# The forget gate's products with the tokens, for two sequences at once, by half-width blocks

## The chip, the cores and the metric

The kernel runs on one core of a Trainium2 chip. The metric is the device time of one execution, in microseconds (us). PE is the matrix engine; its weight loads are listed as PEld and run beside its products. DVE is VectorE, ACT is ScalarE, POOL is GpSimd, and SP issues most of the DMAs. A product here is one matrix instruction: a 128x128 stationary operand (loaded by its own weight load) times a moving operand of up to 512 columns, added up in a PSUM bank. A bank holds 128x512 numbers of 32 bits.

## The reference, cut to what matters

The whole computation is a mixture-of-experts stage, a feed-forward stage chosen by sequence, a second mixture of experts, and a gated recurrence. Only the last one is touched. For x of 32 sequences ("steps" of the scan), each with 128 rows of 512 numbers:

```python
def step(c, xt):
    ft = jax.nn.sigmoid(xt @ wf.T + c @ uf.T + bf)
    it = jax.nn.sigmoid(xt @ wi.T + c @ ui.T + bi)
    gt = jnp.tanh(xt @ wc.T + c @ uc.T + bc)
    c = ft * c + it * gt
    return (c, None)
c_final, _ = lax.scan(step, c0, x)
h = jnp.tanh(jnp.einsum('tbi,oi->tbo', x, wo) + c_final @ uo.T + bo)
return h
```

The input of the scan is r * y: the expert rows y, gathered by token, times sigmoid(r).

## The kernel before

**Precision.** Each 32-bit operand is split into a high part (a cast on ACT) and a remainder (a subtraction on DVE) by `split` (L64, L65). A product of two split operands is made of three products: high by high, high by rest, rest by high (`mm3`, L95). A contraction over 512 numbers has four chunks of 128, so it takes 12 products; over 256 numbers it takes 6.

**The scan** is the loop over t from 0 to 31 near the end of the kernel. Each t multiplies the state c, turned by PE (`turn`) and split into cT, by uc, ui and uf (`from_c`, 36 products of 512 columns into three banks of the pool ps_g). `gate` then adds the token's part, and applies the sigmoid or tanh; `new_c` makes f*c + i*g on DVE, and the next state is turned again. The token parts do not depend on the state. They are placed between `new_c` and the next `from_c`, as filler: some before the turn, while DVE and ACT make the new state, and some behind the turn, while ACT and DVE split it.

**Blocks.** For gates c and i, the token parts of two sequences (a pair n: tokens 2n and 2n+1) are made together. The left operand is seen as 2x2 blocks A11, A12, A21, A22 (sequence by half of the 512 inputs), the right operand as 2x2 blocks (half of the inputs by gate c or i). Instead of eight block products seven are made (Winograd's form of Strassen's method): of A11, A12, A22 and four sums S1 to S4 of A blocks, with B11, B21, B22 and four differences T1 to T4 of B blocks. Each takes 6 products of 512 columns into one of three banks of the pool ps_bF (`block`), and DVE adds the results up. `first_of_pair` makes five of them at odd t, for the even token t+1; `second_i` and `second_c` make the other two at even t. The first pair is done per token, from the block weights (`plain`).

**The forget gate f before the change** is plain: 12 products of 512 columns a token, added to the bank in which `from_c` then puts the state's part.

**Preparing tokens.** `gate_y(b)` multiplies y by sigmoid(r), turns it (ptF), stores it to DRAM for the last stage, and splits it into z; `sums_z` makes S1 to S4 on DVE once both tokens of a pair are there. `get_y` gathers y on POOL's queue and loads r on SP's. The loop does token t+3 at step t.

**Weights.** uc and ui come first, then uf, wc and wi, late in the expert stage. wf comes on POOL's queue during the first products of the scan; the second half of the block weights (`rest_of_weights`) is made at t=0 behind the split of the first new state.

**The end.** Behind the scan wo multiplies all tokens again, four sequences at a time (`unit`, results poF), and the last state's part uo (cu) is added; tanh, an addition and a store follow (`result`). The wo split is at t=28; the uo split is behind the scan.

**Order.** Dependences, semaphores and buffers are handled by a tile framework. Its planner goes through the program and gives each engine, at every point of its own estimate of time, the earliest instruction in the program whose operands and buffer it takes to be ready. So an engine's order is the program's unless something earlier waits: at 2318.57 us the first units of the end stand ahead of the last state's turn. Once it is set, each engine works its list strictly in order. `tc.issue_after` and `queue_behind` put an instruction behind another on the same engine without a wait.

Of the kernel before, what the change touches and what calls it, by code (L numbers as in the profile page):

```python
# [49 lines left out]
def tile_kernel(ctx: ExitStack, tc: tile.TileContext, a: dict, out: bass.AP):  # L50
# [106 lines left out]
    hl = const.tile([P, KD, NB], F32, name="hl")  # L157
# [18 lines left out]
    with ExitStack() as sa:  # L176
# [653 lines left out]
        new_i = po_p.tile([P, NB], I32, name="new_i")  # L830
        ones = po_p.tile([P, P], F32, name="ones2")
# [734 lines left out]
    with sf:  # L1566
# [35 lines left out]
        zp = sf.enter_context(tc.tile_pool(name="zp", bufs=2, **kw))  # L1602

        zA, zS, zts = {}, {}, {}

        def gate_y(b):
# [6 lines left out]
            if j == 0:  # L1613
                z = zp.tile([P, 2 * KD * D], FR, tag="z", name=f"z_{n}")
                zA[n] = z[:, : KD * D].rearrange("p (j h k q) -> p j h k q", j=2, h=2, k=KD)
                zS[n] = z[:, KD * D :].rearrange("p (s h k q) -> p s h k q", s=4, h=2, k=K2)
                zts[n] = first_p.tile([P, 2, KD, P], F32, tag="cT0", name=f"zt_{n}")
# [5 lines left out]
            zt = zts[n][:, j]  # L1623
            if b < LEAD:
                split(zA[n][:, j, 0], zA[n][:, j, 1], pt)
# [3 lines left out]
            if b >= LEAD:  # L1629
                split(zA[n][:, j, 0], zA[n][:, j, 1], zt)  # L1630

        def sums_z(n):
# [3 lines left out]
            s = gp.tile([P, 2, K2, P], F32, tag="sz", name=f"sz_{n}")  # L1636
# [7 lines left out]
        def turn(c, t):  # L1644
            pt = ps_c.tile([P, KD, P], F32, tag="t", name=f"ptC_{t}")
            for k in range(KD):
                nc.tensor.transpose(pt[:, k, :], c[:, bass.ts(k, P)], ident)
# [6 lines left out]

        def block(which, w, n):

            s = {"A11": (0, 0), "A12": (0, 1), "A22": (1, 1)}.get(which)
            if s is None:
                left = zS[n][:, int(which[1]) - 1]
            else:  # L1660
                left = zA[n][:, s[0], :, s[1] * K2 : (s[1] + 1) * K2]
            ps = ps_b.tile([P, D], F32, tag="b", name=f"p{which}_{n}")
            mm3(ps, lambda h, k: left[:, h, k, :], lambda h, k: wt[w][:, h, bass.ts(k, D)], K2)
            return ps

        def plain(t, ps, which, start, stop):
# [5 lines left out]
                "f": ((0, "f0"), (1, "f1")),  # L1672
# [3 lines left out]
            for m, (half, w) in enumerate(todo):  # L1676
                z = zA[n][:, j, :, half * K2 : (half + 1) * K2]
# [6 lines left out]
        half_done, made = {}, []  # L1684

        def first_of_pair(n):

            first, second, c1 = (zop.tile([P, 2, D], F32, tag="raw", name=f"{x}_{n}") for x in ("ta", "tb", "pa"))
            p1, u, v = first[:, 0], first[:, 1], second[:, 0]
            nc.vector.tensor_tensor(p1, block("A11", "B11", n), bias["c"], ALU.add)  # L1690
# [27 lines left out]
        def gate(t, n, ps, v, more):  # L1718
            v[n] = gp.tile([P, D], F32, tag="v" + n, name=f"v_{n}_{t}")
# [5 lines left out]
        def new_c(t, v, c):  # L1725
# [5 lines left out]

        wt = {
            n: wx_p.tile([P, 2, K2 * D], FR, tag="w" + n, name=f"w{n}_hl")
            for n in ("T4", "T3", "T2", "f1", "B22", "T1", "B21", "B11", "f0")
# [167 lines left out]
        for o in range(KD):  # L1902
            unit(0, o)
# [117 lines left out]
```

## Time and profile before

| | us |
|---|---|
| median of three executions | 2417.46 (2416.41 to 2418.44) |
| the profiled execution's own time | 2420.01 |
| its span, first to last instruction | 2418.3 |
| scan, 1781.3 to 2318.3: PE busy | 535.7 of 537.0 |
| scan: DVE busy, ACT busy | 339.6, 169.2 |
| one steady pair of tokens (start of ps_c at 1898.40 to 1931.61) | 33.2 |
| DVE busy in a steady pair (2000.41 to 2033.62) | 20.8 |
| after the scan, 2318.3 to 2418.3: PE busy | 93.6 of 100.0 |

The granted clock of PE is 1.00 in the scan. A row of the profile names the line, the engine, the operation, its output and inputs by the program's names, the shapes and a count. Matrix instructions overlap in their records, so the distance between the starts of two rows tells what a product costs, not its own duration (388 ns for 512 columns, 279 ns for 256). DVE takes 0.69 us for an addition of 128x512 and 0.42 us for one of 128x256.

### The profile page before, as it was taken

The numbers are of one execution on the slowest core, as the hardware profiler recorded it, in microseconds if no ns is written. First come the engines' busy times: TensorE is split into PE (matmuls) and PEld (weight loads), VectorE is DVE, ScalarE is ACT, GpSimd is POOL, SyncE is SP. The second block draws the span as 40 slices with busy tenths as digits, with TensorE's granted clock in tenths as the row PEclk, the third lists the DMA queues.
The fourth block names the chain that finished last, engine by engine and source line by source line (L and its number), as shares of the span: only waits on it lengthen the run. The fifth ranks groups of instructions, "written<-read, shape, count | busy, mean of one in ns | idle before, by whom it ended". The sixth has DMA issues, their size and how long they took to land.

```text
span 2418.3 us, 36797 instructions
## 1 busy us (share of the span) xinstructions
PE 2392.4 (99%) x12792; PEld 2026.3 (84%) x12792; DVE 1484.2 (61%) x2548; ACT 1077.0 (45%) x1897; POOL 422.4 (17%) x461
## 2 busy tenths in 40 slices
PE   9999999999999999999999999999999999999999
PEld 6788788888887888888888889999988888888887
DVE  8896644456557445446355477776756666666664
ACT  5544533343223545445455466666643223223242
POOL 1000022222233233323222120000011000000012
PEclk9999999999999999999999999999999999999999
DMA  6545555457565344343243287777642111111175
GB/s 220 152 128 171 183 170 167 153 184 254 178 216 164 126 129 127 106 133 109 81 153 125 90 288 257 224 229 232 199 153 65 49 44 53 49 44 48 53 235 183
DMA packets 196382, 357.93 MB, mean 148 GB/s; under 512 B 37664, under 2 KB 70480, under 8 KB 193632
## 3 DMA queue, kind: packets, MB, share of 16 engines
q1 hardware_dynamic: 148224, 258.57, 32.8%
q0 software_dynamic: 36448, 75.95, 11.0%
q10 hardware_dynamic: 11520, 20.98, 2.4%
q8 instruction: 107, 1.75, 0.3%
q14 instruction: 83, 0.68, 0.1%
HBM read 377.08 MB, written 91.80 MB: 194 GB/s over the span
## 4 chain that ended last, share of the span: by engine, by line
PE 76%; DVE 2%; DMA 2%; issue 1%; ACT 1%; ACTq 0%; SPq 0%; POOL 0%; DVEq 0%; POOLq 0%
PE po L95 7%; PE phD L95 7%; PE poD L95 7%; PE ps_f L95 7%; PE p L95 6%; PE pb L95 4%; PE ps_i L95 4%; PE ps_c L95 4%; PE poF L95 3%; PE pS L95 3%; PE pv L95 3%; PE acc L95 3%; PE pA L95 2%; PE pur L95 2%; PE por L95 2%
## 5 line engine op out<-in xcount | busy, mean ns | idle before, releaser
L65 DVE TENSOR_TENSOR wD<-rawD,wD 128x1024 fp32r<-128x1024 f32 x128 | 156.3, 1228 | 79.2 <-ACT wD L64 79.1
L95 PE MATMUL p<-xhl,swu 128*128 128x512 f32 x768 | 188.4, 397 | 5.9 <-ACT xhl L64 5.9
L95 PE MATMUL p<-xhl,kept_u 128*128 128x512 f32 x768 | 184.6, 394 | 1.3 <-DVE kept_u L65 0.7
L95 PEld LDWEIGHTS phD<-xe,wD 128*128 128x128 f32 x1536 | 183.2, 188 | 1.3
L95 PE MATMUL phD<-xe,wD 128*128 128x256 f32 x1536 | 183.5, 279 | 0.0
L95 PE MATMUL poD<-wD,hD 128*128 128x512 f32 x768 | 181.9, 392 | 0.7 <-DVE hD L65 0.7
L95 PEld LDWEIGHTS p<-xhl,swu 128*128 128x128 f32 x768 | 144.2, 190 | 36.1 <-ACT xhl L64 5.9
L95 PEld LDWEIGHTS p<-xhl,kept_u 128*128 128x128 f32 x768 | 141.8, 188 | 31.4 <-DVE kept_u L65 1.1
L95 PEld LDWEIGHTS poD<-wD,hD 128*128 128x128 f32 x768 | 141.8, 188 | 29.4 <-DVE hD L65 1.2
L64 ACT CAST wD<-rawD 128x1024 fp32r<-128x1024 f32 x128 | 133.4, 1047 | 54.3 <-PE poD L95 30.8
L305 POOL DMA_INDIRECT xg<-in_x_rows_dram,blk_t x71 | 68.2, 961 | 439.0 <-PE ptx L315 242.8
L1587 POOL DMA_INDIRECT y<-res_d,gat_i x32 | 37.1, 1158 | 471.3 <-DVE r L1612 388.3
L95 PE MATMUL pur<-r,xb 128*128 x792 | 110.6, 288 | 3.5 <-issue 1.5
L65 DVE TENSOR_TENSOR xb<-ptx,xb 128x512 fp32r<-128x512 f32 x68 | 47.0, 691 | 104.5 <-ACT xb L64 101.7
L95 PE MATMUL por<-r,hbr 128*128 x396 | 107.6, 407 | 0.5 <-ACT hbr L64 0.5
L95 PEld LDWEIGHTS pur<-r,xb 128*128 128x128 f32 x792 | 98.5, 188 | 5.6 <-issue 2.4
L95 PE MATMUL ps_c<-uc_hl,cT 128*128 128x512 f32 x384 | 96.3, 399 | 0.0
L95 PE MATMUL pb<-rT,Wo_hl 128*128 128x256 f32 x768 | 94.7, 281 | 0.3 <-DVE rT L65 0.2
L95 PE MATMUL acc<-swd,as 128*128 128x512 f32 x384 | 94.5, 391 | 0.2 <-DVE as L65 0.2
L95 PE MATMUL ps_f<-wf_hl,z 128*128 128x512 f32 x384 | 94.5, 394 | 0.0
L95 PE MATMUL acc<-kept_d,as 128*128 128x512 f32 x384 | 93.6, 392 | 0.8 <-ACT as L64 0.4
L844 POOL DMA_INDIRECT o<-o_d,s_i x64 | 64.5, 1008 | 165.4 <-PE pth L864 71.3
(1048 smaller groups left out, 5137.2 us busy)
## 6 DMA issues: line engine op xcount, KB each, us to landing
rawD<-in_w_key_dram SPq DMA_DIRECT2D x64, 512.0 KB
rawD<-in_w_value_dram SPq DMA_DIRECT2D x64, 512.0 KB
swr<-in_sw_dram SPq DMA_DIRECT2D x120, 256.0 KB
o_d<-obr SPq DMA_DIRECT2D x66, 256.0 KB
rraw<-in_rw_dram SPq DMA_DIRECT2D x32, 256.0 KB
xc<-in_x_dram SPq DMA_DIRECT2D x32, 256.0 KB
hid_d<-o ACTq DMA_DIRECT2D x32, 256.0 KB
xh_d<-xc SPq DMA_DIRECT2D x32, 256.0 KB
```

The source lines that it names most:

```text
L64: first = nc.scalar.copy(hi, src).ins
L65: done = nc.vector.tensor_tensor(lo, src, hi.bitcast(F32), ALU.subtract).ins
L95: done = nc.tensor.matmul(ps, lhsT=left(hl, k), rhs=right(hr, k), start=start and k + n == 0, stop=stop and 3 * k + n == last,)
L305: nc.gpsimd.indirect_dma_start(out=xg[i], out_offset=None, in_=a["x_rows"], in_offset=bass.IndirectOffsetOnAxis(ap=blk_t[:, i : i + 1], ax ...
L844: nc.gpsimd.indirect_dma_start(out=o[n], out_offset=None, in_=o_d, in_offset=bass.IndirectOffsetOnAxis(ap=idx[:, b : b + 1], axis=0),)
L1587: got = nc.gpsimd.indirect_dma_start(out=y, out_offset=None, in_=res_d, in_offset=bass.IndirectOffsetOnAxis(ap=gat_i[:, b : b + 1], axis=0),)
```

## The change

The f gate's token part is made by the same seven blocks. The left blocks are those of the pair, already there for c and i. The right operand is wf alone, its 512 columns cut in two halves: f11, f12, f21, f22 (half of the inputs by half of the columns), with differences T1 to T4 of their own. So each block product is 6 products of 256 columns, and two of them share a bank (`blocks_f`).

- `f_start(n)` makes A11 and A12 of f for pair n. It is run at even t for the next pair (at t=1 for the first one), ahead of the turn; DVE adds its results behind the state's split.
- `f_first(n)` makes S1, S2 and S4 at odd t, behind the turn; its additions go behind the new state.
- `f_second(n)` makes S3 at even t ahead of the turn, and `f_third(n)` makes A22 behind the turn and behind the c block.
- `plain_f` does tokens 0 and 1 one by one, 30 products of 256 columns each, from the block weights.
- The token part of f now reaches the gate as a tile in SBUF (`fs`), as those of c and i did; the state's product with uf starts its own bank.
- The wf weights are prepared as seven half-width blocks in one tile, which starts 64 bytes off (`shifted`); the raw wf lies in the buffer that S1 to S4 of the tokens use later, which has a single copy now.
- The block A21 of a token pair is no longer split except for the first pair. `sums_z` uses the gathered y tile as its scratch, so the next `get_y` comes behind it.
- At the end, the two pools of the scan are closed at t=30 instead of behind the loop. The wo split moves to t=30; two of the four loads of the first group's tokens go to another buffer at t=28 and two are at t=30; the uo split goes behind the last new state, the second group's split behind the first's, and the last state's turn behind the second unit of wo.
- A small tile (hl) moves from a lasting pool to one of an earlier stage.

```diff
         def gate_y(b):
             n, j = divmod(b, 2)
             with tc.issue_after(last_split[1]) if b == 1 else nullcontext():
                 nc.vector.tensor_tensor(r, y, r, ALU.mult)
             if j == 0:
-                z = zp.tile([P, 2 * KD * D], FR, tag="z", name=f"z_{n}")
-                zA[n] = z[:, : KD * D].rearrange("p (j h k q) -> p j h k q", j=2, h=2, k=KD)
-                zS[n] = z[:, KD * D :].rearrange("p (s h k q) -> p s h k q", s=4, h=2, k=K2)
+                zA[n] = zp.tile([P, 3, 2, K2, P], FR, tag="z", name=f"z_{n}")
                 zts[n] = first_p.tile([P, 2, KD, P], F32, tag="cT0", name=f"zt_{n}")
...
+            def split_tokens(t):
+                if j == 0:
+                    t = t.rearrange("p (a k) q -> p a k q", a=2)
+                    split(zA[n][:, 0:2, 0], zA[n][:, 0:2, 1], t)
+                    return
+                if n == 0:
+                    a21.append(gp.tile([P, 2, K2, P], FR, tag="a21", name="a21"))
+                    split(a21[0][:, 0], a21[0][:, 1], t[:, :K2])
+                split(zA[n][:, 2, 0], zA[n][:, 2, 1], t[:, K2:])
...
         def sums_z(n):
             zt = zts[n]
             a1, a2 = zt[:, 0, :K2], zt[:, 0, K2:]
             b1, b2 = zt[:, 1, :K2], zt[:, 1, K2:]
-            s = gp.tile([P, 2, K2, P], F32, tag="sz", name=f"sz_{n}")
+            zS[n] = zp.tile([P, 4, 2, K2, P], FR, tag="zs", bufs=1, name=f"zs_{n}")
+            s = spare[2 * n + 1].rearrange("p (s k q) -> p s k q", s=2, k=K2)
             nc.vector.tensor_tensor(s[:, 0], b1, b2, ALU.add)
             nc.vector.tensor_tensor(s[:, 1], s[:, 0], a1, ALU.subtract)
             split(zS[n][:, 0:2, 0], zS[n][:, 0:2, 1], s)
...
+        def left_of(which, n):
+            if which[0] == "S":
+                return zS[n][:, int(which[1]) - 1]
+            return tokens(n, int(which[1]) - 1, int(which[2]) - 1)
...
+        def blocks_f(n, *todo):
+
+            ps = ps_b.tile([P, 2, HD], F32, tag="b", name=f"pf{todo[0][0]}_{n}")
+            for i, (which, w) in enumerate(todo):
+                left = left_of(which, n)
+                mm3(ps[:, i], lambda h, k: left[:, h, k, :], lambda h, k: wf[w][:, h, k, :], K2)
+            return ps
+
+
+        fs, f_done = {}, {}
+
+        def f_tile(t):
+            pool, tag = (gp, "vf") if t % 2 or t == 0 else (first_p, "c0")
+            fs[t] = pool.tile([P, D], F32, tag=tag, name=f"v_f_{t}")
+            return fs[t][:, :HD], fs[t][:, HD:]
+
+        def plain_f(t):
+            n, j = divmod(t, 2)
+            f_tile(t)
+            ps = ps_b.tile([P, 2, HD], F32, tag="b", name=f"pf_{t}")
+            for i, todo in enumerate((((0, "B11"), (1, "B21")), ((0, "B11"), (0, "T1"), (1, "B22")))):
+                for m, (half, w) in enumerate(todo):
+                    z = tokens(n, j, half)
+                    done = mm3(
+                        ps[:, i], lambda h, k: z[:, h, k, :], lambda h, k: wf[w][:, h, k, :], K2,
+                        m == 0, m == len(todo) - 1,
+                    )
+            nc.vector.tensor_tensor(fs[t], ps.rearrange("p i n -> p (i n)"), bias["f"], ALU.add)
+            return done
+
+        def f_start(n):
+
+            f1, p1 = f_tile(2 * n)
+            ps = blocks_f(n, ("A11", "B11"), ("A12", "B21"))
+            return [
+                nc.vector.tensor_tensor(p1, ps[:, 0], bias["f"][:, :HD], ALU.add).ins,
+                nc.vector.tensor_tensor(f1, ps[:, 1], p1, ALU.add).ins,
+            ]
+
+        def f_first(n, room):
+
+            u, v = room[:, :HD], room[:, HD:]
+            p1 = fs[2 * n][:, HD:]
+            ps = blocks_f(n, ("S1", "T1"), ("S2", "T2"))
+            last = blocks_f(n, ("S4", "B22"))
+            with tc.issue_after(made[0]):
+                nc.vector.tensor_tensor(v, ps[:, 0], bias["f"][:, HD:], ALU.add)
+                nc.vector.tensor_tensor(u, ps[:, 1], p1, ALU.add)
+                nc.vector.tensor_tensor(v, v, u, ALU.add)
+                nc.vector.tensor_tensor(p1, last[:, 0], v, ALU.add)
+            f_done[n] = u, v
+
+        def f_second(n):
+            f1, f2 = f_tile(2 * n + 1)
+            u, v = f_done.pop(n)
+            ps = blocks_f(n, ("S3", "T3"))
+            adds = [
+                nc.vector.tensor_tensor(u, ps[:, 0], u, ALU.add).ins,
+                nc.vector.tensor_tensor(f2, ps[:, 0], v, ALU.add).ins,
+            ]
+            return (f1, u), adds
+
+        def f_third(n, f1, u):
+            nc.vector.tensor_tensor(f1, blocks_f(n, ("A22", "T4"))[:, 0], u, ALU.add)
...
         def first_of_pair(n):
 
             first, second, c1 = (zop.tile([P, 2, D], F32, tag="raw", name=f"{x}_{n}") for x in ("ta", "tb", "pa"))
             p1, u, v = first[:, 0], first[:, 1], second[:, 0]
+            rooms[n] = second[:, 1]
...
         def gate(t, n, ps, v, more):
-            v[n] = gp.tile([P, D], F32, tag="v" + n, name=f"v_{n}_{t}")
+            v[n] = fs.pop(t) if n == "f" else gp.tile([P, D], F32, tag="v" + n, name=f"v_{n}_{t}")
...
+        names = ("T4", "T3", "T2", "B22", "T1", "B21", "B11")
+        f_all = shifted(wx_p, len(names) * K2 * D, tag="wf", name="wf_hl")
+        f_all = f_all.rearrange("p (w h k n) -> p w h k n", w=len(names), h=2, k=K2)
+        wf = {n: f_all[:, i] for i, n in enumerate(names)}
         wt = {
             n: wx_p.tile([P, 2, K2 * D], FR, tag="w" + n, name=f"w{n}_hl")
-            for n in ("T4", "T3", "T2", "f1", "B22", "T1", "B21", "B11", "f0")
+            for n in names
         }
...
         for n in "cif":
-            from_c(0, n, ps, cT, True, False)
-
-
-        f01 = zp.tile([P, 2 * KD * D], F32, tag="z", name="raw_wf")
-        f01 = [f01[:, bass.ts(h, K2 * D)] for h in range(2)]
+            from_c(0, n, ps, cT, True, n == "f")
+
+
+        raw_f = zp.tile([P, KD, D], F32, tag="zs", bufs=1, name="raw_wf")
         with tc.issue_after(first_got):
             for h in range(2):
-                nc.gpsimd.dma_start(out=f01[h], in_=a["wf"].rearrange("p k n -> p (k n)")[:, bass.ts(h, K2 * D)])
+                s = slice(h * K2, (h + 1) * K2)
+                nc.gpsimd.dma_start(out=raw_f[:, s], in_=a["wf"][:, s])
...
         with behind(first_z):
-            for h in range(2):
-                split_part(f"f{h}", f01[h])
+            split_f("B11", f11)
+            split_f("B21", f21)
+            nc.vector.tensor_tensor(f12, f12, f11, ALU.subtract)
+            split_f("T1", f12)
+            split_f("B22", f22)
...
+            nc.vector.tensor_tensor(f22, f22, f12, ALU.subtract)
+            split_f("T2", f22)
+            nc.vector.tensor_tensor(f11, f22, f11, ALU.subtract)
+            nc.vector.tensor_tensor(f21, f21, f22, ALU.subtract)
+            split_f("T3", f11)
+            split_f("T4", f21)
...
                 with tc.issue_after(done):
-                    plain(0, ps, "f", False, True)
+                    plain_f(0)
+                more["f"] = fs[0]
                 for n in "cif":
                     gate(t, n, ps, v, more[n])
             else:
+                more["f"] = fs[t]
                 for n in "cif":
                     from_c(t, n, ps, cT, n not in ps, True)
...
             if t == 1:
 
                 nc.vector.tensor_tensor(bias["i"], bias["i"], bias["c"], ALU.subtract)
+                b1, b2 = (bias["f"][:, bass.ts(i, HD)] for i in range(2))
+                nc.vector.tensor_tensor(b2, b2, b1, ALU.subtract)
             n, odd = divmod(t + 1, 2)
             if t == 0:
                 for w in "ci":
                 cT_next = turn(c, t + 1)
                 with behind(last_split):
                     rest_of_weights()
-                plain(1, ps, "f", True, False)
+                plain_f(1)
             elif t < NB - 1:
                 if odd:
                     second_i(n)
-                    plain(t + 1, ps, "f", True, False)
+                    rest, adds = f_second(n)
+                    if n + 1 < NB // 2:
+                        adds += f_start(n + 1)
                 else:
                     first_of_pair(n)
+                    if n == 1:
+                        f_start(n)
                 cT_next = turn(c, t + 1)
                 if odd:
+
+                    for i in adds:
+                        queue_behind(i, last_split[1])
                     second_c(n)
+                    f_third(n, *rest)
                 else:
-                    plain(t + 1, ps, "f", True, False)
+                    f_first(n, rooms.pop(n))
...
                 gate_y(b)
+                if b % 2:
+                    sums_z(b // 2)
+                spare.pop(b)
                 if b + LEAD < NB:
                     get_y(b + LEAD)
-                if b % 2:
-                    sums_z(b // 2)
...
             if t == NB - 4:
-
-                wo1 = zp.tile([P, 2, KD, D], FR, tag="z", name="wo_hl")
+                raws = []
                 for k in range(KD):
-                    raw = yp.tile([P, D], F32, tag="yr"[k % 2], name=f"raw_wo{k}")
+                    raws.append(yp.tile([P, D], F32, tag="yr"[k % 2], name=f"raw_wo{k}"))
                     with tc.issue_after(last_r[0]):
-                        nc.sync.dma_start(out=raw, in_=a["wo"][:, k, :])
+                        nc.sync.dma_start(out=raws[k], in_=a["wo"][:, k, :])
+                first_z = first_p.tile([P, 2, KD, P], F32, tag="cT0", name="zr_0")
+                first_z = [first_z[:, j] for j in range(2)]
+                for j in range(2):
+                    nc.sync.dma_start(out=first_z[j], in_=z_d[0][j])
+            if t == NB - 2:
+
+                sx.close()
+                sz.close()
+                op = sf.enter_context(tc.tile_pool(name="op", bufs=1, side="right", **kw))
+                zp = sf.enter_context(tc.tile_pool(name="z0p", bufs=1, **kw))
+                uo1 = op.tile([P, 2, KD * D], FR, tag="uo", name="uo_hl")
+                wo1 = op.tile([P, 2, KD, D], FR, tag="wo", name="wo_hl")
+                for k, raw in enumerate(raws):
                     split(wo1[:, 0, k], wo1[:, 1, k], raw)
-                first_z = []
-                for j in range(GB):
+                for j in range(2, GB):
                     first_z.append(yp.tile([P, KD, P], F32, tag="yr"[j % 2], name=f"zr_0_{j}"))
                     nc.sync.dma_start(out=first_z[j], in_=z_d[0][j])
-        sx.close()
-        op = sf.enter_context(tc.tile_pool(name="op", bufs=1, side="right", **kw))
...
         split_z(0)
-        uo1 = op.tile([P, 2, KD * D], FR, tag="uo", name="uo_hl")
-        for h in range(2):
-            s = bass.ts(h, K2 * D)
-            split(uo1[:, 0, s], uo1[:, 1, s], raw_part("uo", h))
+        first_z = tuple(last_split)
+        with behind(first_z), tc.issue_after(made[0]):
+            for h in range(2):
+                s = bass.ts(h, K2 * D)
+                split(uo1[:, 0, s], uo1[:, 1, s], raw_part("uo", h))
...
-        for o in range(KD):
-            unit(0, o)
+        ahead = [unit(0, o) for o in range(KD)]
+        for i in turned_c:
+            queue_behind(i, ahead[1])
...
         for g in range(NG):
             if g + 1 < NG:
-                split_z(g + 1)
+                with behind(first_z) if g == 0 else nullcontext():
+                    split_z(g + 1)
```

## The prediction

> **What bounds the kernel now.** First the page's head, its table of busy time, and one group of instructions:
>
> ```profile
> span 2418.3 us, 36797 instructions
> PE 2392.4 (99%) x12792; PEld 2026.3 (84%) x12792; DVE 1484.2 (61%) x2548; ACT 1077.0 (45%) x1897; POOL 422.4 (17%) x461
> ...
> L95 PE MATMUL ps_f<-wf_hl,z 128*128 128x512 f32 x384 | 94.5, 394 | 0.0
> ```
>
> The matrix engine (PE) is busy in 99% of the span. The change rewrites the 384 products of the third line. They lie in the scan, 1781 to 2318 us. So the second view is PE's timeline over one steady token there (column one is the start, column two the extent of the row):
>
> ```profile
> 2003.36 2.88 PE L95 MATMUL ps_f<-uf_hl,cT 128*128 128x512 f32 x12
> 2006.08 1.52 PE L95 MATMUL pS<-wT_hl,z 128*128 128x512 f32 x6
> 2007.44 2.89 PE L95 MATMUL ps_f<-wf_hl,z 128*128 128x512 f32 x12
> 2010.16 0.60 PE L1647 MATMUL ptC<-ident,c 128*128 128x128 f32 x4
> 2010.52 1.64 PE L95 MATMUL pA<-wT_hl,z 128*128 128x512 f32 x6
> 2011.99 0.60 PE L1620 MATMUL ptF<-ident,r 128*128 128x128 f32 x4
> 2012.35 3.01 PE L95 MATMUL ps_c<-uc_hl,cT 128*128 128x512 f32 x12
> ```
>
> No row has a wait. The extents overlap, so a product costs the distance of starts: 12 in 2.72 us, 226.7 ns each. The same view in the expert stage prices a 256-column product, which the change will use:
>
> ```profile
> 1620.12 11.47 PE L95 MATMUL phD<-xe,wD 128*128 128x256 f32 x96
> 1631.43 2.92 PE L95 MATMUL poD<-wD,hD 128*128 128x512 f32 x12
> ```
>
> 96 in 11.31 us: 117.8 ns, which is 52% of 226.7, not 50%. Third, what the filler between the state's products covers. VectorE (DVE) in the same token:
>
> ```profile
> 2008.39 0.69 DVE L1728 TENSOR_TENSOR c<-v_f,v_i 128x512 f32<-128x512 f32 x1
> 2009.00 0.68 DVE L1705 TENSOR_TENSOR ta<-pS,ta 128x512 f32<-128x512 f32 x1
> 2009.60 0.68 DVE L1706 TENSOR_TENSOR pd<-pS,tb 128x512 f32<-128x512 f32 x1
> ...
> 2011.41 0.69 DVE L65 TENSOR_TENSOR cT<-ptC,cT 128x512 fp32r<-128x512 f32 x1 [1.13 <-ACT cT L64]
> ```
>
> The new state is ready at 2009.08 and PE turns it at 2010.16, its weight load 0.23 earlier: 0.85 us to spare. Queued 512-column additions start 0.60 apart. Last, the start of the scan, where DVE is full, and PE's only wait of the scan, from the table of waits:
>
> ```profile
> 1809.81 0.69 DVE L65 TENSOR_TENSOR cT<-ptC,cT 128x512 fp32r<-128x512 f32 x1 [1.98 <-ACT cT L64]
> ...
> 1825.96 0.68 DVE L1690 TENSOR_TENSOR ta<-pA,bc_bc 128x512 f32<-128x512 f32 x1
> ...
> 1826.70 1.65 PE L95 MATMUL pS<-wT_hl,z 128*128 128x512 f32 x6 [0.21 <-DVE ta L1690]
> ```
>
> ```profile
> PE pS L95 <- DVE ta L1690: 0.2, 1, 0.2
> ```
>
> There PE waited for a PSUM bank of the block pool (three banks), which `ta` frees.
>
> **The change, part by part.** The profiled execution took 2420.01 us (span 2418.3), 2.55 above the median of three; I sum differences against it and set them on the median.
>
> *Products of pairs 1 to 15.* Out go 2 × 12 products of 512 columns: 24 × 0.2267 = 5.44 us a pair. In come 7 blocks of 6 products of 256 columns: 42 × 0.1178 = 4.95. That is 0.49 × 15 = **−7.4 us**, all on the path because PE never idles.
>
> *The rule against it.* The Trainium skill, "TensorE: Matmul & The Clock Gate", section "Back-to-back issue gap", gives sustained spacings of about 131 ns for 512 columns and 81 for 128 in streams of weight load and product; in between, 256 would cost an estimated 98, and 42 × 98 against 24 × 131 would be a loss of 0.97 us a pair, 14.6 in all. This trace has 226.7 and 117.8, so the change wins by the trace; only the rule's direction remains, that a narrower product costs more per column.
>
> *Seams.* A 512-column row straight after 256-column ones took 2.76 instead of 2.72 (from 1631.43 to 1634.19). One to three such seams a pair, 0.04 each: 0.6 to 1.8; I take one, since two of the three meet transposes, which cost what they did: **+0.6**.
>
> *The first pair* stays per token but by the block weights, 12 + 18 products of 256 columns: 60 × 0.1178 = 7.07 against 5.44: **+1.6**, half of it before the first turn of the state.
>
> *Weights of f.* Out: two casts and two subtractions of 1024 columns on ACT and DVE. In: seven of each of 512 columns, and four subtractions of whole blocks. The first four with one subtraction lie at 1793 to 1799, where DVE idled 0.95 and 0.79 us before its two rows for wf: nothing; uncovered, 0.6. The last three with three subtractions, (3 + 3) × 0.60 = 3.6 us of DVE, go behind the state's split at 1810, into the full queue shown above.
>
> *What that delays.* `ta` must come behind 3.6 of weights, 0.60 (the plain f sum of token 1), 0.34 (the bias difference; 128x256 ones in the queue are 0.34 apart, as 1822.89 and 1823.22), less 0.26 for half a token split: 4.3, and DVE starts 0.8 later because PE turns later. So `ta` ends at 1826.64 + 5.1 = 1831.7. PE ends the state's products 1.6 later than now, at 1822.5, and has banks for A11, A12 (2.72) and the new two-block start (1.41), then four transposes (0.36): 1827.0. Wait 4.7, less the 0.2 of now: 4.5. Below, the bound is 0, if DVE takes `ta` early; above, 6, if activations hold it up too. DVE idled 0.76 in this stretch for ACT, which new work fills: **+3.7**.
>
> *Additions.* Nine of 128x256 a pair, 9 × 0.34 = 3.1, less 0.26 for the halved split of the odd token (its first half is no longer needed; ACT saves 0.25). In the steady 33.2 us DVE is busy 20.8; it becomes 23.6. Cover: DVE's gaps; five of the nine fall in the odd half, where DVE is full from 2013.25 to 2018.8 and the gates v_i and v_f then have 2.3 us before PE turns the state. Cost nothing; without cover, up to 1.5 a pair.
>
> *Filler before the odd turn* shrinks from 18 wide products (4.08) to 6 wide and 18 narrow (3.48): the 0.85 in hand becomes 0.25. Nothing, but it is what is late next. After the turn it grows by 0.71. At the even turn, 30 wide products (6.8) stay ahead, and 18 narrow ones (2.1) instead of 12 wide (2.7) behind; the state's split ends 1.6 us before its products there, and about 1.0 then: nothing.
>
> *Banks at the odd turn.* S3, f's S3 and the next pair's start hold all three block banks. The c block A22 needs S3's, free after `pd` at 2010.28, against 2009.95 when PE comes; f's A22 needs the bank whose two sums are queued behind the state's split, about 2012.2 against 2011.8. Program order would wait 0.4 + 0.5. But ptF (0.36) and the next ps_c are ready, and this order is planned by readiness: at 1792 to 1795 ps_c, ps_i and ptF alternate. Between 0 and 0.9 × 14 = 12.6: **+0.5**, nearest the rows of now, which have no wait.
>
> *Moves.* The row gather (POOL) of every other token waits for the sums, which use its buffer: about 16 us later (2002.4 to 2018.2), and read at 2034.7; the next gather behind it on POOL was at 2017.65: nothing. SP's load of r and store of z keep their order. The scratch tile move issues nothing.
>
> *End.* The split of wo (four casts, 2.4 us of ACT and DVE each) goes from token 28 to 30, behind the freed weights (2312); two of the group's four loads wait for its buffers and land about 2.6 us after issue (as r: issued 2012.62, used 2015.24), then four splits (2.5): done near 2317.7, PE comes at 2318.5. SP's later loads, zr, x1, queue behind them by 3 to 4 us; first use 2328, covered. uo's split goes behind the last state, needed at 2330.7. PE now idles 0.84 for the last state's turn (2323.87); the turn is put behind two units (5.4 us), which hides it. Between −0.84 and +2: **−0.4**.
>
> Sum: −7.4 + 0.6 + 1.6 + 3.7 + 0.5 − 0.4 = −1.4; 2417.46 − 1.4 = **2416.1 us**.
>
> **Rivals.**
>
> *The start does not wait.* DVE takes `ta` in a gap, as it did at 1825.96, between the gate's product and the new state. Against it: that gap came only once the queue was empty. A wait of 0.5, no bank waits and the whole 0.84: −7.4 + 0.6 + 1.6 + 0.5 − 0.84 = −5.5: 2412.0.
>
> *The banks of the odd turn.* Slower: PE stays in program order there and waits 0.9 at each of 14 turns, 12.6 instead of 0.5: 2428.2. It decides from 0.5 us a turn: (4.8 + 1.4 + 0.5)/14. For it: three banks, all held; against it: PE's alternation at 1792.
>
> *The end comes late.* The two loads take 8.1 us, as zr at 2309 in the chain of waits, 5.5 longer, and PE waits some 4.7: 2421.2, more with a longer start.
>
> **How the numbers follow.** Chances: forecast 0.38 (its own range 2412.5 to 2421), no wait at the start 0.33, banks 0.23, end 0.06. About 0.2%, 4.8 us, is what a measurement can tell. Faster: 0.30 of the first rival and 0.04 of the forecast; slower: 0.21 of the banks, 0.04 of the end, 0.03 of the forecast; the rest within. The range, 2410.8 to 2428.5, reaches the first two rivals and leaves out about one case in ten above, where several bounds meet, and one in twenty below.
>
> **What would show it.** Rows with wf: 690 products of 256 columns near 118 ns; more, and the first term falls. The steady pair: 33.21 becomes about 32.8; 33.5 means bank waits, and the table of waits would have PE at A22 behind DVE. Between 1820 and 1835 PE should wait some 4 us for `ta`; none is the first rival. PE's 0.84 before the last turn goes. Wrong altogether: if DVE's odd half delays v_f by over 2 us.

## The result: slower by 0.4%, and the profile after

The changed kernel took 2426.96 us (median of six runs, 2423.45 to 2431.24), the kernel before 2417.95 (six runs, 2414.04 to 2419.27): a ratio of 1.004, with a 95% interval of 1.003 to 1.005. The forecast was 2416.1 and no change. The profiled execution of the changed kernel took 2431.24 us, 10.2 us more of span than the one of before.

The page of the changed kernel, its head and its table of busy time; the table of groups by shape, the products with wf; and PE's timeline over an odd turn:

```profile
span 2428.5 us, 37608 instructions
PE 2398.3 (99%) x13098; PEld 2043.0 (84%) x13098; DVE 1535.5 (63%) x2696; ACT 1075.7 (44%) x1903; POOL 417.7 (17%) x461
```

```profile
L95 PE MATMUL pfS<-wf_hl,zs 128*128 128x256 f32 x360 | 48.5, 283 | 0.0
L95 PE MATMUL pfA<-wf_hl,z 128*128 128x256 f32 x270 | 36.5, 279 | 0.0
...
L95 PE MATMUL pf<-wf_hl,z 128*128 128x256 f32 x42 | 5.4, 280 | 0.0
```

```profile
2014.86 0.87 PE L95 MATMUL pfS<-wf_hl,zs 128*128 128x256 f32 x6
2015.57 1.57 PE L95 MATMUL pfA<-wf_hl,z 128*128 128x256 f32 x12
2016.99 0.60 PE L1667 MATMUL ptC<-ident,c 128*128 128x128 f32 x4
2017.42 0.38 PE L1627 MATMUL ptF<-ident,r 128*128 128x128 f32 x2
2017.77 1.66 PE L95 MATMUL pA<-wT_hl,z 128*128 128x512 f32 x6
2019.26 0.38 PE L1627 MATMUL ptF<-ident,r 128*128 128x128 f32 x2
2019.40 0.71 PE L95 MATMUL ps_c<-uc_hl,cT 128*128 128x512 f32 x2
```

The products are the narrow ones that were forecast, 12 in 1.42 us, and the odd turn has no wait. So the loss must lie elsewhere. I cut the span at four rows of PE's timeline: the first product of ps_c in the scan, the first of token 2, the first of token 30, and the first product of poF behind cu.

| stage, us | before | after | difference | forecast |
|---|---|---|---|---|
| up to the scan | 1781.57 | 1782.42 | +0.85 | 0 |
| start: tokens 0 and 1 | 50.17 | 58.46 | +8.29 | +6.1 |
| 14 steady pairs | 464.58 | 459.81 | −4.77 | −5.8 |
| end: token 30 to poF behind cu | 39.96 | 43.49 | +3.53 | −1.7 |
| the rest of the end | 82.02 | 84.32 | +2.30 | 0 |

(The forecast's column shares its own terms out: 36 wide products for 90 narrow ones, +2.44, and the wait of 3.7 at the start; −0.49 a pair, and the seams and banks, in the pairs; 12 wide for 12 narrow, −1.31, and −0.4 at the end.) The code before the scan is the same in both but for the place of the small tile hl, and the executions shown below differ there by up to 5.4 us (1777.20 to 1782.60); I take that row for drift between executions. The pairs gained nearly what they should: 33.18 us became 32.84. Start and end lost 14.1, where 4.4 had been forecast.

At the start, the table of waits (of PE, 1775 to 1850) and PE's timeline:

```profile
PE ptC L1667 <- DVE c L1817: 2.5, 1, 2.5
...
PE pS L95 <- DVE zs L65: 0.2, 1, 0.2
```

```profile
1830.98 1.12 PE L1667 MATMUL ptC<-ident,c 128*128 128x128 f32 x4 [2.49 <-DVE c L1817]
1831.92 2.93 PE L95 MATMUL pS<-wT_hl,zs 128*128 128x512 f32 x6
1834.64 2.64 PE L95 MATMUL pS<-wB_hl,zs 128*128 128x512 f32 x6
1837.12 1.52 PE L95 MATMUL pfA<-wf_hl,z 128*128 128x256 f32 x12
```

There is a wait where the forecast had one, 2.7 us in all, though nearly all of it is for the state (c) and not for `ta`. But what follows was not forecast: six products of 512 columns take 2.72 us (1831.92 to 1834.64), and not 1.36. PE runs at half its clock. At the end the same is seen, around cu (timeline of all engines, four of its PE and two of its ACT rows):

```profile
2335.14 2.79 PE L95 MATMUL cu<-cT,uo_hl 128*128 128x128 f32 x24
2336.03 2.18 ACT L64 CAST zF<-zr 128x512 fp32r<-128x512 f32 x4 [5.08 <-DMA zr<-z_d]
...
2338.12 0.36 ACT L2041 ACTIVATE cu<-cu,bo_sb 128x128 f32<-128x128 f32 x1
2338.53 2.63 PE L95 MATMUL cu<-cT,uo_hl 128*128 128x128 f32 x12 [0.60 <-ACT cu L2041]
...
2341.57 2.82 PE L95 MATMUL cu<-cT,uo_hl 128*128 128x128 f32 x12 [0.41 <-ACT cu L2041]
...
2344.18 8.19 PE L95 MATMUL poF<-zF,wo_hl 128*128 128x512 f32 x25
```

ACT stands at a cast zF, which waits for its load, with the first activation of cu queued behind it; cu's two banks are not freed, and PE waits 0.60 and 0.41. Behind the first pause twelve products take 2.63 us, where 24 had taken 2.79. cu as a whole takes 9.04 us against 5.31 before.

The third view gives the clock. It is the table of busy time by stretches; its columns are PE, PEld, DVE, ACT and POOL busy, then the granted clock of PE, the share of the DMA engines, and GB/s. The stretches are cut at 3.41 us, where the clock was found to change:

```profile
1826.80:1830.21 3.41, 1.47 (x6) 0.67 (x4) 3.41 (x7) 1.16 (x3) 0.00 (x0) 1.00 0.00 0
1830.21:1833.62 3.41, 2.64 (x8) 2.13 (x9) 3.41 (x7) 0.59 (x1) 2.38 (x2) 0.50 0.23 55
1833.62:1837.04 3.42, 3.42 (x9) 2.65 (x9) 2.20 (x5) 0.00 (x0) 0.06 (x1) 0.50 0.31 98
...
2335.38:2338.80 3.42, 2.82 (x25) 2.68 (x25) 2.11 (x4) 2.44 (x5) 0.00 (x0) 1.00 0.87 295
2338.80:2342.21 3.41, 3.00 (x15) 2.82 (x15) 2.96 (x6) 2.62 (x6) 0.00 (x0) 0.50 0.45 166
2342.21:2345.62 3.41, 3.41 (x15) 3.12 (x15) 2.71 (x5) 2.10 (x5) 1.58 (x1) 0.50 0.58 225
2345.62:2349.04 3.42, 3.42 (x10) 2.65 (x9) 0.91 (x2) 0.63 (x1) 1.28 (x1) 0.50 0.78 199
```

In before the clock is 1.00 from the scan's start to the last product. Here five cells of 3.41 us run at 0.50. PE was busy in them for 6.06 us at the start and 9.83 at the end; half of that, 3.0 and 4.9 us, is lost to the clock. The other executions agree: the mean granted clock is 0.996 to 0.998 in the six runs of the changed kernel, and 0.999 to 1.000 in all 37 runs of the kernel before that stand beside the experiments. So the theory to test: the change makes PE stand still in two places, for some 2.7 and 1.0 us, and each time the clock takes more than the wait did.

### The profile page after: what moved, and what is told of

Its sections match the earlier page's. It is cut to its first block, busy times and chain, and to the rows that moved or that the text cites. A ratio compares the mean times of both kernels' runs of the same rounds, so it can differ in the third digit from the quotient of the medians.

```text
span 2428.5 us, 37608 instructions
## 1 busy us (share of the span) xinstructions
PE 2398.3 (99%) x13098; PEld 2043.0 (84%) x13098; DVE 1535.5 (63%) x2696; ACT 1075.7 (44%) x1903; POOL 417.7 (17%) x461
## 4 chain that ended last, share of the span: by engine, by line
PE 75%; DVE 3%; DMA 2%; issue 1%; ACT 1%; ACTq 0%; POOL 0%; DVEq 0%; SPq 0%; POOLq 0%
PE phD L95 7%; PE poD L95 7%; PE po L95 7%; PE p L95 6%; PE pb L95 4%; PE ps_i L95 4%; PE ps_c L95 4%; PE poF L95 3%; PE pS L95 3%; PE ps_f L95 3%; PE pv L95 3%; PE acc L95 3%; PE pA L95 3%; PE pfS L95 2%; PE pur L95 2%; PE por L95 2%
## 5 line engine op out<-in xcount | busy, mean ns | idle before, releaser
L64 ACT CAST wD<-rawD 128x1024 fp32r<-128x1024 f32 x128 | 133.6, 1047 | 53.7 <-PE poD L95 31.0
L95 PE MATMUL pv<-w_recept_hl,xr 128*128 128x512 f32 x384 | 93.0, 391 | 0.0
```

The source lines that it names most:

```text
L64: first = nc.scalar.copy(hi, src).ins
L95: done = nc.tensor.matmul(ps, lhsT=left(hl, k), rhs=right(hr, k), start=start and k + n == 0, stop=stop and 3 * k + n == last,)
```

## The experiments

The times of all runs, each against runs of the kernel before on the same chip, and the stages of each profiled execution. In the last two kernels some products of token 2 (in late_f two each of ps_c and ps_i and one of ps_f) are drawn ahead of the rest, so that the row where the start stage ends can't be compared; start and pairs are therefore added.

| kernel | median us | before | ratio (95%) | up to the scan | start + pairs | end | rest | cells at half clock, scan and end |
|---|---|---|---|---|---|---|---|---|
| before | 2417.95 | | | 1781.57 | 514.75 | 39.96 | 82.02 | 0 |
| changed | 2426.96 | 2417.95 | 1.004 (1.003–1.005) | 1782.42 | 518.27 | 43.49 | 84.32 | 2 + 3 |
| start_fill | 2424.98 | 2417.86 | 1.0029 (1.0018–1.0041) | 1779.41 | 515.96 | 41.89 | 83.64 | 0 + 1 |
| end_cu_first | 2421.01 | 2417.86 | 1.0014 (1.0004–1.0024) | 1782.60 | 517.41 | 39.64 | 82.05 | 1 + 0 |
| pool_subs | 2429.69 | 2417.86 | 1.005 (1.0033–1.0067) | 1781.35 | 518.04 | 43.33 | 84.38 | 1 + 3 |
| late_f2 | 2418.39 | 2418.53 | 0.9999 (0.999–1.0008) | 1777.20 | 513.64 | 39.72 | 82.04 | 0 + 0 |
| late_f | 2417.29 | 2418.53 | 1.0 (0.9991–1.0009) | 1778.02 | 513.47 | 39.71 | 82.10 | 0 + 0 |

**Does a wait of PE alone bring the half clock?** The kernel before, made to wait:

```diff
             ...
+            for k in range({4: 6, 6: 6, 8: 6, 10: 8, 12: 8, 14: 8, 16: 8, 18: 10, 20: 10, 22: 10}.get(t, 0)):
+                nc.vector.tensor_tensor(v["f"], v["f"], v["i"], ALU.subtract if k % 2 else ALU.add)
             c = new_c(t, v, c)
```

> This is the kernel before, with pairs of additions and subtractions put on DVE ahead of ten of its states (every second turn from t=4 to t=22), so that PE has to wait for a state: six, eight or ten extra operations of about 0.72 us, which by the order of work leave waits of about 1.8 us (three turns), 3.2 us (four) and 4.7 us (three). What is computed is the same but for rounding. Theory (the clock follows what PE did in one cell of a fixed grid of time, and goes to half for whole cells): low clock only behind some of the waits; every fall and every rise lies on one grid of 3.41 us (the step that the two low stretches of the changed kernel's profile have: 1830.20 to 1837.03 and 2338.76 to 2349.02, 2 and 3 steps long, their beginnings 149.0 steps apart); the 4.7 us waits trip it always, the 3.2 us ones in about half of the cases, the 1.8 us ones hardly ever; the span grows by the 32 us of waits and by some 20 us of half clock, to about 2470 us. Rival (the clock fell for something else in the changed kernel, its narrower products or the busier DVE): clock 1.00 throughout, about 2450 us.

It took 2453.93 us (one run; before 2417.86), less than expected, for the waits came out shorter than planned: none at t=4 to 8, 1.70 us (and another 0.67 behind the turn) at t=10 to 16, 3.84 at t=18 to 22. All seven brought the half clock, the short ones too. Two of the seven turns on PE's timeline, and the cells around them:

```profile
1980.12 0.66 PE L1647 MATMUL ptC<-ident,c 128*128 128x128 f32 x4 [1.70 <-DVE c L1730]
```

```profile
2132.09 1.11 PE L1647 MATMUL ptC<-ident,c 128*128 128x128 f32 x4 [3.84 <-DVE c L1730]
```

```profile
1977.56:1980.97 3.41, 1.52 (x10) 0.92 (x9) 3.41 (x7) 1.11 (x3) 0.00 (x0) 1.00 0.67 231
1980.97:1984.39 3.42, 2.94 (x7) 2.36 (x8) 3.25 (x7) 1.67 (x3) 0.00 (x0) 0.50 0.02 5
...
2127.75:2131.16 3.41, 0.50 (x5) 0.26 (x3) 3.41 (x8) 1.25 (x2) 0.00 (x0) 1.00 0.62 211
2131.16:2134.57 3.41, 2.40 (x7) 1.80 (x8) 3.38 (x7) 1.22 (x2) 1.15 (x1) 0.50 0.23 70
2134.57:2137.99 3.42, 3.42 (x9) 2.65 (x9) 3.14 (x6) 1.51 (x3) 0.70 (x1) 0.50 0.02 10
```

The seven falls, from 1980.95 to 2209.64, are 37.55 us apart or, once, 40.96, which is 11 and 12 steps of 3.413 us, and each stretch lasts one or two steps: the grid holds. The rival's narrow products fall as the cause, since this kernel has none of them. Its other half, a busier DVE, this run does not exclude, since the added operations are on DVE; the next one does, where DVE's list at the start is the changed kernel's and the clock stays up. My expectation that short waits hardly ever trip it falls too, with a proviso: the turns with a short wait are 37.4 to 37.5 us apart, 10.9 to 11.0 steps, so the four met the grid at nearly the same point, and it was one at which the whole wait lies in one cell. The bill of the scan and end, +37.5 us against before, is 21.0 of waits, 13.4 of half clock (PE busy 26.7 us in nine such cells), and 3.1 that I did not break down.

**Is the loss at the start wait or clock?** The wait filled with products that nobody reads:

```diff
+                        warm = bank("warm", t)
+                        for _ in range(12):
+                            mm(warm, zA[0][:, 0, 0, 0, :], wt["B11"][:, 0, bass.ts(0, D)], True, True)
```

> The changed kernel with twelve more products of 512 columns, whose result nobody reads, at the turn t=1 where PE waits for DVE: four beside the first sums' products, eight ahead of the turn of the states. They cost PE 12 x 226.7 ns = 2.7 us, of which some 1.8 fit into the wait. Theory (half of the loss at the start is the clock, tripped by the wait): the granted clock stays at 1.00 between 1826 and 1840, the products behind the turn take 1.36 us for six and not 2.7, and from the first row of ps_c to that of t=2 the stage takes 55 to 56.5 us in place of 58.46, though PE does more; time 1 to 3 us below the changed kernel's 2427. Rival (DVE bounds the stage, the slow products are hidden beside it): clock 1.00 too, but the stage takes 58.3 to 59.5 us, and the time is the same or up to 1 us longer.

PE's timeline of start_fill (the rows ps_warm are the added products):

```profile
1825.58 1.97 PE L56 MATMUL ps_warm<-wB_hl,z 128*128 128x512 f32 x8
1827.91 0.66 PE L1667 MATMUL ptC<-ident,c 128*128 128x128 f32 x4 [0.36 <-DVE c L1817]
1828.85 1.65 PE L95 MATMUL pS<-wT_hl,zs 128*128 128x512 f32 x6 [0.28 <-DVE ta L1779]
1830.34 1.52 PE L95 MATMUL pS<-wB_hl,zs 128*128 128x512 f32 x6
```

Six products take 1.36 us again (1830.34 to 1831.70), the clock stays at 1.00, and the start takes 56.18 us, 2.3 less than in the changed kernel, with 2.7 us more work on PE. DVE's queue did not bound the stage behind the wait; the clock did. The time, 2424.98, is 2 us below the changed kernel's, as expected, but the runs of the two overlap (2421.80 to 2428.13 here), so that the evidence is the stage and not the time.

**What holds the end?** Only ACT's order is changed:

```diff
-            nc.scalar.activation(cu[:, o, :], pc, AF.Identity, bias=bo1[:, o : o + 1])
+            cu_done = nc.scalar.activation(cu[:, o, :], pc, AF.Identity, bias=bo1[:, o : o + 1]).ins
...
-                with behind(first_z) if g == 0 else nullcontext():
+                with behind(first_z) if g == 0 else tc.issue_after(cu_done):
```

> The changed kernel with one order changed on ACT: the casts zF of the second and later groups of the end stand behind the last activation of cu, and no longer ahead of it, where they wait for a transfer. Theory (cu's two banks are held up by ACT's order, and PE's pauses there trip the clock): the products of cu take about 5.3 to 5.7 us in place of 9.04, clock 1.00 between 2336 and 2350, from ps_c of t=30 to the first poF behind cu 39.9 to 40.3 us in place of 43.49, the rest 82.0 to 82.5 in place of 84.32; time 4 to 6 us below the changed kernel's. Rival (the end is late for its transfers, the order on ACT only shows it): the waits move from cu to poF, stage and rest together stay within 1 us of 127.8, time the same as the changed kernel's.

The rows of cu and the first one behind it, all engines' timeline of end_cu_first:

```profile
2334.34 5.47 PE L95 MATMUL cu<-cT,uo_hl 128*128 128x128 f32 x48
2335.89 0.37 ACT L2041 ACTIVATE cu<-cu,bo_sb 128x128 f32<-128x128 f32 x1 [5.74 <-PE cu L95]
...
2339.65 8.66 PE L95 MATMUL poF<-zF,wo_hl 128*128 128x512 f32 x37
```

All 48 products of cu in one row without a wait, 5.31 us as before; the end is 39.64 (39.96 before; a little below what was expected) and the rest 82.05 (82.02). That is 6.1 us back in the profile, and 6.0 in the median (2421.01). Nothing was late but the order: the casts behind cu cost PE nothing.

**Is it DVE's queue that makes PE wait at the start?** First the six subtractions that combine weights in rest_of_weights, moved from DVE to POOL (one of them shown):

```diff
-            nc.vector.tensor_tensor(i1, i1, i0, ALU.subtract)
+            nc.gpsimd.tensor_tensor(i1, i1, i0, ALU.subtract)
...
```

> The changed kernel with the six subtractions that combine the weights of c and i and of f made on POOL and no longer on DVE: DVE has about 5.2 us less in its queue at the scan's start. Theory (the wait at t=1 is DVE's queue, and the half clock is that wait's): no wait of PE for c above 0.7 us there, clock 1.00, from the first row of ps_c to that of t=2 51.8 to 52.6 us (before's 50.17 and the 1.63 of the first pair's products) in place of 58.46; time 5 to 7 us below the changed kernel's. Rival (the weights are late whoever combines them: POOL's slower rows make PE wait for wT or wB in place of c): waits of 2 us or more for weights, stage 54 to 59 us, time within 3 us of the changed kernel's.

2429.69 us, no better than the changed kernel: the rival's outcome, though not for its reason. The wait for the state is gone; in its place PE waits for the very first weights of f, whose difference and splits DVE makes late (table of waits, 1780 to 1845; then POOL's and DVE's rows):

```profile
PE pf L95 <- ACT wf_hl L64: 1.9, 1, 1.9
PE pf L95 <- DVE wf_hl L65: 1.5, 1, 1.5
```

```profile
1796.44 2.74 POOL L1885 TENSOR_TENSOR raw_wc<-raw_wc,raw_wi 128x1024 f32<-128x1024 f32 x1
1796.85 2.88 DVE L65 TENSOR_TENSOR wf_hl<-raw_wf,wf_hl 128x512 fp32r<-128x512 f32 x1
...
1799.14 2.83 POOL L1886 TENSOR_TENSOR raw_wc<-raw_wi,raw_wc 128x1024 f32<-128x1024 f32 x1
...
1799.65 2.86 DVE L1874 TENSOR_TENSOR raw_wf<-raw_wf 128x512 f32<-128x512 f32 x1
```

An operation of DVE that takes 0.68 us elsewhere takes 2.88 beside one of POOL. The experiment moved the wait, and with it a half-clock cell (1805.02 to 1808.44, behind one with 0.38 us of PE busy). The turn of t=1 has no wait here and no half clock, but the time did not tell, and so it did not decide the question.

Second, on top of end_cu_first, DVE's order alone. What the state of t=1 does not need goes behind it; no work is taken away (t2 to t4 lie in the raw tiles of i):

```diff
             if t == 1:
-                nc.vector.tensor_tensor(bias["i"], bias["i"], bias["c"], ALU.subtract)
+                with tc.issue_after(made[0]):
+                    split_f("T2", rest_f[0])
+                    nc.vector.tensor_tensor(bias["i"], bias["i"], bias["c"], ALU.subtract)
...
+            nc.vector.tensor_tensor(t2, f22, f12, ALU.subtract)
+            nc.vector.tensor_tensor(t3, t2, f11, ALU.subtract)
+            nc.vector.tensor_tensor(t4, f21, t2, ALU.subtract)
...
                     f_first(n, rooms.pop(n))
+                    if n == 1:
+                        with behind(last_split):
+                            split_f("T3", rest_f[1])
+                            split_f("T4", rest_f[2])
```

> The kernel of end_cu_first (the changed kernel with the end's casts behind cu) with DVE's order at the start changed, too, and no work taken away: the three combined weights of f (T2, T3, T4) are summed into the free buffers of i's raw weights, T2's split and the change of the two rows of bias wait for the state of t=1, the splits of T3 and T4 stand behind the first f_first. Ahead of that state DVE has three splits and one subtraction less, 4 x 0.60 us = 2.4 us. Theory (the wait at t=1 is DVE's queue ahead of the state, and the half clock comes of the wait): PE's waits there 0 to 1.7 us in all and the clock at 1.00; from the first row of ps_c to that of t=2 52 to 54.5 us (end_cu_first: 57.6); time 3 to 5.5 us below end_cu_first's 2421.0, 2415.5 to 2418, which is at or below the kernel before. Rival (DVE has too much work in the whole stage, and what is put off is missed later): the wait moves to the products of S4, pfS or S3, which wait for banks or weights, stage 56 us or more, time 2420 to 2422.

In late_f T2's split stays in its place, and the second half of the sums of the next pair is kept back and issued at t=1 behind made[0]:

```diff
             split(zS[n][:, 0:2, 0], zS[n][:, 0:2, 1], s)
+            if n == 1:
+                sums_late.append(lambda: more_sums(n, s, zt))
+            else:
+                more_sums(n, s, zt)
```

> As late_f2, but T2's split stays ahead of the state, and the second half of the sums for the next pair (two sums, one subtraction of a split: 0.34 + 0.34 + 0.60 us) stands behind the state instead: 2 x 0.60 + 0.60 + 1.28 = 3.1 us less ahead of it. Theory (DVE's queue): PE does not wait for the state of t=1 by more than 0.7 us, clock 1.00, stage 52 to 54.5 us, time 2415 to 2418. Rival (too much work in the stage): the products of S4, which need the late sums, and the turn stand still instead, in the order that PE has; 56 us or more, 2420 to 2423.

Both do it. late_f's rows around the turn of t=1 (timelines of DVE and of PE), and all that its table of waits has for PE from 1780 to 1860:

```profile
1823.37 0.68 DVE L1827 TENSOR_TENSOR c<-v_f,v_i 128x512 f32<-128x512 f32 x1
```

```profile
1825.00 0.60 PE L1677 MATMUL ptC<-ident,c 128*128 128x128 f32 x4
1826.27 0.73 PE L95 MATMUL ps_c<-uc_hl,cT 128*128 128x512 f32 x2 [0.67 <-ACT cT L64]
```

```profile
PE ps_c L95 <- ACT z L64: 0.7, 1, 0.7
PE ps_c L95 <- ACT cT L64: 0.7, 1, 0.7
PE ptF L1627 <- DVE r L1621: 0.4, 1, 0.4
```

The state is ready 0.95 us before PE turns it, no cell runs at half clock, and what was put off is not missed. Less the changed kernel's pairs (459.8) the start is 53.8 us in late_f2 and 53.7 in late_f, inside what was expected; late_f2's time is 0.4 us above it. Start and pairs take 513.47 us in late_f: 3.9 less than in end_cu_first, 1.3 less than before. The medians, 2418.39 and 2417.29, fell by 2.6 and 3.7 us against end_cu_first, which ran on another chip (3.3 and 4.4 if each is set against the kernel before on its own chip); against the kernel before they are 0.1 and 1.2 us lower, which the intervals do not tell from no change. This is the best version that the runs found: the change costs nothing any more, and it brings nothing that can be measured.

## Why the prediction was wrong

- *Products of pairs 1 to 15* (−7.4) *and of the first pair* (+1.6): right. There are 630 products pfS and pfA and 60 of pf, about 118 ns apart (12 in 1.42 us above).
- *Seams* (+0.6): too small. The pairs gained 4.77 us where the products alone give 14 × 0.49 = 6.9, so they cost 2.1, 0.15 a pair. The odd turn has it: ptC takes 0.43 us and ptF, which is cut in two, 0.35 and 0.14, where each took 0.36 in one piece. That is 0.20 more; the rest of the pair is 0.05 shorter than reckoned.
- *Banks at the odd turn* (+0.5, and the rival with 12.6): no wait. The table of waits has no row there, because PE takes ptF and A22 in turns, as the forecast argued; what that order costs is the cut of ptF, counted above.
- *Filler before the odd turn, additions, moves* (nothing): no wait in the steady pairs; the state was in the end ready 0.5 us before its turn (2016.51 against 2016.99).
- *What the weights of f delay* (+3.7, worked 4.5): place and cause were right, and late_f shows that it is DVE's queue. PE waited 2.7 us, for the state itself and not for `ta`. But this step failed: it took a wait to cost its own length. The 3.0 us of half clock that the wait brought appear in none of its terms, nor in a rival. (A slip beside it: the 0.2 us for `ta` were not PE's only wait in before's scan. PE also waited 0.4 us for ptF at 1790.27 and 0.7 for ps_c at 1791.60; the changed kernel has both, too, and the sum does not use them.)
- *End* (−0.4, bounds −0.84 to +2): this is the step that failed worst; end and rest together were to change by −1.7 and changed by +5.8. "SP's later loads … queue behind them by 3 to 4 us; first use 2328, covered" looked only at who uses the loads, and was too small: the first two were issued at 2314.27 and 2317.04 and no longer at 2309.09 and 2309.57, the next at 2330.76 and no longer at 2321.95, 8.8 us later. The first user of that one is a cast on ACT (2336.03 above), ACT works in order, and the activation of cu that frees PE's banks was queued behind it. 1.0 us of waits came of that and, with the narrow products of cu, 4.9 of half clock. The wait of 0.84 for the last turn did go, but waits for zF and cT (0.6 + 0.2 + 0.3) took its place. With ACT's order mended (end_cu_first), end and rest are 0.29 us shorter than before, and not 1.7: the waits for zF and cT stay (0.7 and 0.3), and I did not break down the rest.
- *The sum*: the forecast's −1.4 is about what late_f, without the two stalls, gives: −1.2 in the median, −1.45 in the sum of the stages from the scan on (−1.28 − 0.25 + 0.08). Its parts are not the forecast's, though: the seams cost more and the start less, so that the two totals agree is luck.

Of the changed kernel's +10.2 us of span, then: −5.7 products, +7.9 half clock, +2.5 more waits at the start and +1.3 at the end, +0.85 drift, and 3.4 that remain, of which 2.1 are the seams of the pairs and 1.3 stay open.

## What to carry to other kernels

On an engine that is busy 99% of the time, price a new wait of PE by what the clock does after it, too: here 2.7 us of waiting cost 3.0 more, and two pauses of 0.6 and 0.4 among narrow products cost 4.9. When a load is moved later, follow not only its first user but all that stands behind that user on its in-order engine. When work is added before a state that everything waits for, put what the state does not need behind it: order alone gave back here all that the change had lost.

## What the hardware showed that was not expected

**The clock goes by cells of a fixed grid.** In every profile that has low stretches, all of them in one execution begin at the same point of a 3.413 us step, whatever the code does, and, but for the one behind the last product, which runs to the end of the trace, last a whole number of steps; two executions have different points (0.19 of a step in the changed kernel, 0.36 in gaps, 0.59, 0.76 and 0.81 in end_cu_first, start_fill and pool_subs). So the same wait can cost more or fewer cells from one execution to the next. The start of end_cu_first is the changed kernel's in code and has the same wait of 2.5 us, but one cell where that has two; the end of start_fill has one where the changed kernel has three, though PE waits 1.6 us in its cu and not 1.0. I take this for a reason why the changed kernel's runs spread over 7.8 us; no run was made for it.

A cell with PE busy 1.52 us or less was followed by half clock in all cases shown. Cells of mostly 512-column products with more than that were not: 1.63 at 2405.36 in late_f2, 2.57 at 2321.53 in before, 2.60 at 2321.73 in the changed kernel. Busy time does not settle it, though. Start_fill, end_cu_first and pool_subs have one half-clock cell at about 101 us, before any changed code, and in the cell ahead of it PE is busy throughout (3.41 us), but some 30 of its 38 or 39 products have only 16 columns; in before these are spread over two cells, and the clock stays. Cells of cu's 128-column products fell at 2.16, 2.37 and 2.82 us busy, while before has one filled with them entirely that kept its clock:

```profile
2331.77:2335.18 3.41, 3.41 (x33) 3.41 (x32) 3.41 (x6) 2.57 (x6) 0.00 (x0) 1.00 0.67 256
```

24 such products take 2.65 us there (48 in 5.31), which is 1160 columns a us, against 2258 for wide ones (512 in 226.7 ns). If the clock goes by columns and not by time, all of this is one threshold near half of what a cell can hold: 1.52 of 3.41 is 45% of it and falls, a cell full of narrow products 51% and stays, one with 2.82 of them 42% and falls. That is worked out from these rows; no run was made for it. To rise again, a cell at half clock needed PE busy for 2.94 us or more with wide products (2.64 did not do), and a cell that held products of cu did not do it with 3.41 us (2342.21).

The Trainium skill, "TensorE: Matmul & The Clock Gate", Part 1, describes a free-running window of 4096 cycles at 1.2 GHz, 3413 ns, after which an idle PE goes to half rate. The step measured here agrees with it. Its table under "Why this matters for your kernels" allows PE idle gaps of up to about 3 us; here a gap of 1.70 us with 0.67 behind it, one of 2.49, and pauses of 0.60 with narrow products around them were enough, and the measurement decides. The same page was cited in the prediction for the spacing of products only.

**DVE waits for POOL.** In pool_subs a subtraction of 128x512 on DVE took 2.88 us beside a POOL operation of 2.74, against 0.68 alone. The Trainium skill, "SBUF — State Buffer", section "SBUF: two separate sides", says that an operation of DVE with two inputs in SBUF and one of GpSimd (POOL) that reads SBUF share a pair of ports: whichever starts first holds it for its whole instruction, and the other blocks. These rows agree: DVE's two end 0.55 and 0.54 us behind the POOL operations that had begun before them.
